# A graph network with experts on one core: edge stages in a fixed order, edge one-hots from ScalarE, and later work moved into them

## The chip, the cores and the metric

The kernel runs on one core of a Trainium2 chip. The metric is the device time of one execution in microseconds; the median of three runs stands for a kernel. A core has five engines with a queue of instructions each: PE (TensorE, matrix products into the accumulator memory PSUM; weight loads are its PEld row), DVE (VectorE), ACT (ScalarE), POOL (GpSimd, which also issues the indirect DMAs that gather rows by index) and SP (SyncE, which issues plain DMAs). [...]

## The reference

Nodes have 256 values each (3125 nodes); 53125 edges (`src`, `dst`) join them. Four layers follow each other, each added to its input, each on a layer norm:

```python
x = x + _L0_gnn_ref(_layernorm(x), edge_index, edge_weight, ...)
x = x + _L0_ffn_ref(_layernorm(x)[None], ...)[0]
x = x + _L1_gnn_ref(_layernorm(x), ..., src, dst, edge_type_200)
x = x + _L1_ffn_ref(_layernorm(x)[None], ...)[0]
```

Layer 0's graph part gives each edge four weights, `w = exp(-relu(score/20))`, where the score is a value of the edge's near node plus one of its far node plus a multiple of the edge's own value; a node receives the weighted mean of its neighbours' features (`pooled / row_sum`). Its experts part sends each node to the best two of 16 experts, each `silu(x w1) * (x w2)` times `w3`. Layer 1's graph part sums `(h[src] + rel_e) @ weight_neighbor * alpha` over the edges into a node, where `alpha = exp(leaky_relu(score))` divided by itself (so it is 1 up to rounding), takes a relu and adds one of two products of the node, by whether edges come in. Its last part gives every node a weight from a router vector, finds the 1561 nodes with the largest weights (`top_k` of half, less one), and for these adds a two-layer gelu network times the weight.

## The kernel before, in words

The kernel (a class, `_Kernel`, run by `run`, L1477) is written against a layer that adds the semaphores and, outside of fixed blocks, arranges the order of instructions on each engine by its own estimate of their times.

**Nodes** are 25 tiles of 128 (`NT`), `x` stays in SBUF. **Edges** are sorted by their near node into 25 buckets, one for each node tile, in 440 tiles of 128 edges (`sort_edges`, L310: `load_in`, `places`, `move`, `load`); 18 tiles make a bucket, handled in groups of `GRP` = 6 tiles, so there are 74 groups (`edge_groups`, L714). `load` (L578) keeps for each edge its far node's index, its row in the bucket and its value, and writes rows (and types, in layer 1) once more to DRAM as rows of bf16 (`wide`).

**An edge stage** is the same for both layers (`edge_stages`, L724, called through `pipelined`, L811). For each group:

- `gather` issues six indirect DMAs on POOL (L754) that fetch the far nodes' rows from a table in DRAM (`table0`, `table1`) into `rows` (3 buffers); at a bucket's head, `spread` has SP fetch the bucket's `wide` row to all partitions (L744); DVE makes `oh`, one-hots of edge by node, from `numbers` in PSUM and the edges' rows (L762); DVE makes the same turned over, `hot`, from `wide` (L771; in layer 1 two more, of relations).
- `message`: PE multiplies `hot` with near values (L780), DVE sums their three parts (L787), and the layer's `messages` makes weights and messages (L916 for layer 0; L1308 for layer 1, where it writes one-hots of the relation behind the gathered row, L1313, and ACT makes `ohw`, the one-hots times the weight, L1319).
- `add`: PE sums one-hots times messages into a bank of `ps_sums` (L798). After a bucket's last group, `acc` is that bank plus `more` (edges that overflowed, a DMA issued there, L804), and `finish` uses it (L933, L1324).

The stages stand one group apart: while group g is gathered, g-1 gets its messages and g-2 is summed. During layer 0's edges `pipelined` takes one piece of layer 1's sorting (`ranking`) per step, and `finish` calls `done` of `gate` (L966), which at the end of five buckets does their layer norm, writes them to `xtab`, and makes the experts' logits.

**After layer 0's edges**, `experts` (L989) routes the nodes, then runs 65 tiles of expert work with layer 1's `move` as filling, then combines: 50 gathers on POOL (L1170), each added to `x` by DVE (L1174). `relations_features` (L1181) then prepares layer 1's weights, norms all tiles and writes `table1` and `near1`; `load` fetches the sorted edges; `relations_edges` (L1272) is layer 1's edge stage. `depths` (L1367) then norms all tiles, makes the router's weights `wc`, turns them into a row, counts for each node how many weights are larger (49 comparisons over up to 3125 values, L1426), and runs the last network in blocks of four tiles (L1453, L1464).

PSUM is one pool for the whole kernel: tag A with 2 buffers of two banks, tag B with 4 of one.

## Time and profile before

| | us |
|---|---|
| median of 3 runs | 2635.79 (2631.52 to 2639.92) |
| the profiled execution's own time | 2845.15 |
| its span, first to last instruction | 2842.8 |
| mean granted PE clock | 0.822 of full speed |

| busy over the span | us | share | instructions |
|---|---|---|---|
| PE matmuls | 1878.6 | 66% | 7534 |
| PE weight loads | 1126.4 | 40% | 7534 |
| DVE | 1446.3 | 51% | 3397 |
| ACT | 390.7 | 14% | 1097 |
| POOL | 1167.4 | 41% | 1198 |

The profile is of one execution. A group's line names the line of the kernel, the engine, the operation, the tile written and those read, the count, then busy time and the mean of one in ns, and after a second bar the engine's idle time just before these instructions with what ended most of it. "issue" means that the profile shows nothing that was waited for, "remote" that what ended the wait isn't known to it. A line of the stretches gives length, busy time and count of PE, PEld, DVE, ACT and POOL, then PE's granted clock, the share of the DMA engines and GB/s. A line of waits gives the total, the number and the longest. The profiled execution took longer than the runs did; a sum of its durations is a sum in its own time.

### The profile page before, as it was taken

The page shows a single profiled execution, that of the slowest core. Times are in us where ns is not written, and L with a number is a line of the kernel's source. Part 1 is how long each engine was busy: PE and PEld are TensorE (multiplying, and loading weights), DVE is VectorE, ACT ScalarE, POOL GpSimd, SP SyncE. Part 2 cuts the span into 40 slices and gives each one's busy share as a digit, 9 for nine tenths or more (in the row PEclk, how much of TensorE's full clock was granted, in tenths as well). Part 3 has the DMA queues.
Part 4 walks back from the last instruction along what each step waited for, and adds up shares of the span by engine and source line. Part 5 has one row for each costly group of instructions (what it writes and reads, how often), then busy time and mean ns, then how long its engine had stood idle before and what let it go on. Part 6 is the DMA issues. An engine that isn't in the chain of part 4 may idle for free.

```text
span 2842.8 us, 24381 instructions
## 1 busy us (share of the span) xinstructions
PE 1878.6 (66%) x7534; PEld 1126.4 (40%) x7534; DVE 1446.3 (51%) x3397; ACT 390.7 (14%) x1097; POOL 1167.4 (41%) x1198
## 2 busy tenths in 40 slices
PE   3169554854544443399999991447878778785298
PEld 0024232543433332356666660323434334343166
DVE  4876225476665343644422224445655556549721
ACT  0000010010000000100112120112222222221012
POOL 4235306576654646034411115036666666650000
PEclk9999996676666667577799996768889888898599
DMA  2000325343444433144499982254545455431000
GB/s 83 0 3 5 104 89 137 93 130 112 115 100 114 116 100 101 49 150 130 131 316 318 317 291 84 87 156 131 148 129 148 130 142 149 128 85 34 8 21 18
DMA packets 258938, 334.04 MB, mean 118 GB/s; under 512 B 30861, under 2 KB 192407, under 8 KB 258807
## 3 DMA queue, kind: packets, MB, share of 16 engines
q1 hardware_dynamic: 197527, 191.26, 21.3%
q0 software_dynamic: 51920, 132.68, 17.6%
q10 hardware_dynamic: 9360, 8.52, 0.9%
q8 instruction: 61, 1.00, 0.1%
q14 instruction: 70, 0.57, 0.1%
HBM read 298.38 MB, written 33.98 MB: 117 GB/s over the span
## 4 chain that ended last, share of the span: by engine, by line
PE 39%; DVE 14%; issue 10%; POOL 9%; another core or an unknown queue 8%; DMA 4%; ACT 1%; SPq 0%; DVEq 0%; POOLq 0%; ACTq 0%
PE ps_sums L798 10%; PE ps_h L1130 9%; POOL rows L754 9%; PE ps_y L1147 4%; PE s_mv L560 3%; DVE cmp L1426 3%; PE ps_hid L1453 3%; PE ps_out L1464 3%; DMA rows<-table,s_idx 3%; DVE msg L926 2%; DVE hot L771 2%; PE ps_x_t L173 1%; PE ps_h_t L173 1%; PE ps_f L1264 1%
## 5 line engine op out<-in xcount | busy, mean ns | idle before, releaser
L754 POOL DMA_INDIRECT rows<-table,s_idx x880 | 848.6, 964 | 725.0 <-issue 240.4
L798 PE MATMUL ps_sums<-msg,oh 128*128 128x260 f32 x880 | 306.6, 519 | 261.8 <-DVE msg L926 143.1
L798 PE MATMUL ps_sums<-rows,ohw 128*128 128x457 f32 x880 | 414.0, 616 | 62.8 <-ACT ohw L1319 54.1
L798 PEld LDWEIGHTS ps_sums<-msg,oh 128*128 128x128 f32 x880 | 226.6, 265 | 325.1 <-issue 250.1
L560 PE MATMUL s_mv<-s_hv,s_hp 128*128 128x200 f16 (+1 forms) x832 | 246.8, 472 | 89.9 <-DVE s_hv L555 89.9
L798 PEld LDWEIGHTS ps_sums<-rows,ohw 128*128 128x128 f32 x880 | 179.0, 215 | 217.5 <-issue 149.6
L1130 PE MATMUL ps_h<-w,x_t 128*128 128x512 f32 x520 | 256.1, 638 | 0.0
L771 DVE TENSOR_SCALAR hot<-wide,pcols 128x768 bf16<-128x768 bf16 (+1 forms) x296 | 175.4, 597 | 73.9 <-PE ps_near L780 63.0
L560 PEld LDWEIGHTS <-s_hp 128*128 128x128 f16 x832 | 122.1, 147 | 208.7 <-issue 180.3
L762 DVE TENSOR_TENSOR oh<-ps_hold,s_row 128x768 f32<-128x768 f32 (+1 forms) x148 | 139.9, 946 | 125.7 <-remote 73.5
L1119 POOL DMA_INDIRECT xg<-xtab,who x65 | 61.9, 952 | 345.1 <-PE ps_x_t L173 302.6
L569 POOL DMA_INDIRECT s_tab<-s_rec,s_to x130 | 147.8, 1137 | 115.1 <-ACT s_rec L566 78.9
L780 PEld LDWEIGHTS <-hot 128*128 128x128 bf16 x1760 | 70.0, 98 | 212.3 <-issue 149.2
L1136 DVE TENSOR_TENSOR hid<-hid,ps_h 128x512 f32<-128x512 f32 x65 | 44.7, 688 | 210.3 <-ACT hid L1135 204.4
L1319 ACT ACTIVATE ohw<-oh,s 128x128 f32<-128x128 f32 x440 | 136.5, 388 | 106.6 <-DVE s L1282 75.2
L1130 PEld LDWEIGHTS ps_h<-w,x_t 128*128 128x128 f32 x520 | 102.8, 209 | 105.7 <-issue 105.5
L926 DVE TENSOR_TENSOR msg<-rows,ps_hold 128x1536 f32<-128x1536 f32 x74 | 128.1, 1731 | 2.0 <-ACT ps_hold L924 1.9
L787 DVE TENSOR_REDUCE near<-ps_near 128x24 f32<-128x72 f32 (+2 forms) x148 | 29.4, 198 | 190.3 <-remote 150.2
L1147 PE MATMUL ps_y<-w,h_t 128*128 128x256 f32 x520 | 122.9, 379 | 0.7 <-ACT h_t L175 0.7
L1147 PEld LDWEIGHTS ps_y<-w,h_t 128*128 128x128 f32 x520 | 98.7, 190 | 41.7 <-issue 30.6
L545 DVE TENSOR_TENSOR s_hp<-num_p,s_pp 128x1024 f16<-128x1024 f16 x104 | 71.8, 690 | 82.8 <-PE s_mv L560 81.4
L1313 DVE TENSOR_TENSOR rows<-ps_hold,s_val 128x1200 f32<-128x1200 f32 x74 | 101.1, 1367 | 6.1 <-PE ps_sums L798 6.1
(307 smaller groups left out, 2344.2 us busy)
## 6 DMA issues: line engine op xcount, KB each, us to landing
w<-in_L_ffn_w_dram SPq DMA_DIRECT2D x195, 512.0 KB
wide<-s_w SPq DMA_DIRECT2D x72, 576.0 KB
rows<-table,s_idx POOLq DMA_INDIRECT x880
ytab<-y ACTq DMA_DIRECT2D x65, 128.0 KB
sums<-sums_z SPq DMA_DIRECT2D x5, 1142.5 KB
more<-sums SPq DMA_DIRECT2D x25, 228.5 KB
sums<-sums_z SPq DMA_DIRECT2D x5, 650.0 KB
table<-f SPq DMA_DIRECT2D x5, 650.0 KB
```

Source lines behind the costliest of these rows:

```text
L560: nc.tensor.matmul(ps[:, : NK * V], hp[:, :, j], rec[:, :, :, j].rearrange("p k v -> p (k v)"), start=(j0 + j == 0), stop=(j0 + j == C - 1),)
L569: d = nc.gpsimd.indirect_dma_start(out=tab, out_offset=bass.IndirectOffsetOnAxis(ap=to[:, i : i + 1], axis=0), in_=out[:, k * CH * V : (k ...
L754: nc.gpsimd.indirect_dma_start(out=rows[:, j, :width], out_offset=None, in_=table, in_offset=bass.IndirectOffsetOnAxis(ap=st["idx"][:, k + ...
L762: nc.vector.tensor_tensor(oh[:, :n, :], numbers[:, None, :P].to_broadcast(sh), st["row"][:, k : k + n, None].to_broadcast(sh), op=OP.is_equal,
L771: nc.vector.tensor_scalar(t[:, : n // 2, :], w, at, None, op0=OP.is_equal)
L798: nc.tensor.matmul(ps[:, :W], oh[:, j, :], msg[:, j, :], start=(head and j == 0), stop=(last and j == n - 1),)
L926: nc.vector.tensor_tensor(msg[:, :n, :HO].rearrange("p j (h o) -> p j h o", o=O), rows[:, :n, :HO].rearrange("p j (h o) -> p j h o", o=O), ...
L1130: nc.tensor.matmul(ph[:, i * HID : (i + 1) * HID], xt[:, c, :], w12[:, i, c, :], start=(c == 0), stop=(c == C - 1),)
L1147: nc.tensor.matmul(py[:, :D], ht[:, c, :], w3[:, c, :], start=(c == 0), stop=(c == HC - 1))
L1313: nc.vector.tensor_tensor(rows[:, :n, R0:], self.numbers[:, None, :R].to_broadcast(sh), st["val"][:, k : k + n, None].to_broadcast(sh), op ...
L1319: nc.scalar.activation(ow[:, j, :], oh[:, j, :], AF.Copy, scale=s[:, 1, j : j + 1])
L1426: nc.vector.tensor_scalar(cmp[:, s:e], wrow[:, s:e], w, None, op0=op, op1=OP.add, accum_out=rank[:, t, i : i + 1],)
```

## The change: what it does

1. **Edge stages.** `edges` takes the place of `edge_stages` and `pipelined`, and inside `tc.manual_schedule()` every engine keeps the order in which the code issues its instructions. A step g issues: the spread of group g+2 (now for each group, two rows of 128 with 8 of padding side by side, so that a group is one run of 1584 bytes), the gathers of g, the closing of a bucket whose last group was g-3, the one-hots and near products of g, the message and the sums of g-1, and a piece of other work, up to 2.2 us by the numbers that the pieces yield. A bucket's `more` is loaded with its first spread. `finish` is a generator and goes on in half steps.
2. **One-hots.** DVE's `oh` comparison goes. ACT makes |row - node| for each tile (`Abs`); in layer 0 a Relu of 1 minus that is the one-hot; in layer 1 the Relu has scale -alpha and bias alpha, and so carries the weight.
3. **Layer 1's relation one-hots** (`prepare`) are written right after the group's gather is issued. `rows` has 4 buffers in layer 1, `oh` 3 in layer 0.
4. **Filling.** The sort's pieces yield 2.6; `gate`'s work is cut into pieces that are queued behind it. The last layer's norm, router weights and counts (`router`, `route`) leave `depths` and become pieces of layer 1's edge stage; a count over all nodes is split by when the nodes are finished. Its weights are loaded ahead of that stage.
5. **Layer 1's features.** Weights are prepared ahead of `experts`; norm and `table1` of four tiles follow as soon as these are combined.
6. **PSUM** is opened anew for each part; in the edge stages it holds two near banks, two separate banks of sums, one held bank and three others.

```diff
     def load():
...
+            wide = [
+                self.dram.tile([MT // 2, 2 * P + 8], BF16, name=f"{name}_w{i}")
+                for i in range(1 + (not bits))
+            ]
...
+        def spread(g):
+            b, k, n, head = groups[g][:4]
+            wide[g] = []
+            for i, w in enumerate(st["wide"]):
+
+                t = pool.tile([P, G // 2, 2 * P + 8], BF16, name=f"wide{i}", bufs=3)
+                src = w[k // 2 : (k + n) // 2, :].rearrange("(o k) r -> o (k r)", o=1)
+                nc.sync.dma_start(
+                    t[:, : n // 2, :].rearrange("p k r -> p (k r)"),
+                    src.to_broadcast([P, n // 2 * (2 * P + 8)]),
+                )
+                wide[g].append(t[:, : n // 2, : 2 * P])
             if head:
-                now[b] = [spread(i, b) for i in range(len(st["wide"]))]
-            rows = pool.tile([P, G, into], F32, name="rows", bufs=3)
+                more[b] = pool.tile([P, W], F32, name="more")
+                nc.sync.dma_start(more[b], sums[b])
+
+        def gather(g):
+            k, n = groups[g][1:3]
+            rows = pool.tile([P, G, into], F32, name="rows", bufs=self.rows_bufs)
...
-            oh = pool.tile([P, G, P], F32, name="oh", bufs=3)
-            nc.vector.tensor_tensor(
-                oh[:, :n, :], numbers[:, None, :P].to_broadcast(sh),
-                st["row"][:, k : k + n, None].to_broadcast(sh), op=OP.is_equal,
-            )
...
+            far = pool.tile([P, G, P], F32, name="off", bufs=2)
+            for j in range(n):
+                nc.scalar.activation(
+                    far[:, j, :], self.iota[:, :P], AF.Abs, scale=-1.0,
+                    bias=st["row"][:, k + j : k + j + 1],
+                )
+            pe = self.ps("near", "ps_near")
...
+        def close(b):
+            acc = pool.tile([P, W], F32, name="acc")
+            nc.vector.tensor_add(acc, bank.pop(b)[:, :W], more.pop(b))
+            yield from finish(b, acc)
...
+        with tc.manual_schedule():
+            spread(0)
+            spread(1)
+            for g in range(len(groups) + 3):
+                if g + 2 < len(groups):
+                    spread(g + 2)
+                if g < len(groups):
+                    rows = gather(g)
+                if g >= 3 and groups[g - 3][4]:
+                    closers.append(close(groups[g - 3][0]))
+                go_on()
+                if g < len(groups):
+                    live[g] = rows, *hots(g)
+                    if prepare:
+                        prepare(*groups[g][1:3], rows)
+                if 0 <= g - 1 < len(groups):
+                    message(g - 1)
+                go_on()
+                piece(2.2)
+            while closers:
+                go_on()
+            piece(1e9)
...
-            def messages(k, n, rows, near, oh):
+            def messages(k, n, rows, near, off):
+                oh = pool.tile([P, G, P], F32, name="oh", bufs=self.oh_bufs)
+                nc.scalar.activation(oh[:, :n, :], off[:, :n, :], AF.Relu, bias=1.0, scale=-1.0)
...
-                done(b)
...
+                self.queue.append(done(b))
+                yield
...
-    def experts(self, fill):
+    def experts(self, fill, done):
...
+                done(t)
...
+            ends = list(range(4, NT - 4, 4)) + [NT - 3, NT]
+
+            def done(b):
+                if b + 1 not in ends:
+                    return
+                i = ends.index(b + 1)
+                t0, t1 = ends[i - 1] if i else 0, b + 1
+                self.norm_tiles(self.h1, t0, t1)
...
+                nc.vector.tensor_scalar(s[:, 2, :n], s[:, 1, :n], -1.0, None, op0=OP.mult)
                 ow = pool.tile([P, G, P], F32, name="ohw", bufs=3)
                 for j in range(n):
                     nc.scalar.activation(
-                        ow[:, j, :], oh[:, j, :], AF.Copy, scale=s[:, 1, j : j + 1]
+                        ow[:, j, :], oh[:, j, :], AF.Relu,
+                        bias=s[:, 1, j : j + 1], scale=s[:, 2, j : j + 1],
                     )
...
+        def route(b):
+            if b + 1 not in ends:
+                return
+            i = ends.index(b + 1)
+            t0, t1 = ends[i - 1] if i else 0, b + 1
+            for _ in self.norm_pieces(z, t0, t1):
+                yield 1.2
...
+            end = min(N, t1 * P)
+            for t in range(t0):
+                count(t, t0 * P, end, OP.is_gt, 3 + i)
+                if t % 3 == 2:
+                    yield 2.2
+            for t in range(t0, t1):
+                lo, hi = t * P, min(N, (t + 1) * P)
+                count(t, 0, lo, OP.is_ge, 0)
+                count(t, lo, end, OP.is_gt, 1)
...
+                yield 2.2
...
+        general = dict(A=2, B=4)
+        at_edges = dict(near=2, sums=2, hold=1, B=3)
...
+                    self.rows_bufs, self.oh_bufs = 3, 3
                     self.heads_edges(st, ranking, self.gate(pool))
-                with tc.tile_pool(name="move1", bufs=1) as moves:
-                    self.experts([lambda f=f: f(moves) for f in steps])
-        self.relations_features()
-        self.relations_edges(load())
-        self.depths()
+                with self.banks(**general):
+                    features = self.relations_features()
+                    with tc.tile_pool(name="move1", bufs=1) as moves:
+                        self.experts([lambda f=f: f(moves) for f in steps], next(features))
+                        next(features, None)
+                    st = load()
+        with tc.tile_pool(name="route", bufs=1) as pool:
+            with self.banks(**at_edges):
+                self.router(pool)
+                self.rows_bufs, self.oh_bufs = 4, 2
+                self.relations_edges(st)
+            with self.banks(**general):
+                self.depths()
```

## The prediction

> **What bounds the kernel now.** I read the page's busy shares first, then the mean of each stage, then what the gathers cost and wait for, then who waits longest in the two edge stages. No engine is full over the span:
>
> ```profile
> PE 1878.6 (66%) x7534; PEld 1126.4 (40%) x7534; DVE 1446.3 (51%) x3397; ACT 390.7 (14%) x1097; POOL 1167.4 (41%) x1198
> ```
>
> So each stage has its own limit. Stages, from the busy times by stretch: layer 0's edges, the experts alone, combining plus layer 1's tables, layer 1's edges, and the last layer.
>
> ```profile
> 429.00:1169.00 740.00, 384.03 (x1586) 282.81 (x1586) 410.72 (x967) 51.54 (x190) 432.66 (x440) 0.68 0.40 109
> ...
> 1420.00:1718.00 298.00, 295.38 (x1120) 185.53 (x1118) 78.33 (x153) 61.33 (x103) 42.54 (x45) 1.00 0.90 299
> 1718.00:1871.00 153.00, 41.37 (x186) 29.46 (x186) 67.89 (x200) 9.86 (x27) 47.65 (x51) 0.68 0.29 90
> 1871.00:2557.00 686.00, 525.91 (x2486) 266.08 (x2487) 379.81 (x959) 171.97 (x587) 415.89 (x440) 0.86 0.50 137
> 2557.00:2843.00 286.00, 192.64 (x716) 129.52 (x714) 148.32 (x313) 50.12 (x83) 0.29 (x1) 0.85 0.06 20
> ```
>
> Columns: length, then busy time of PE, weight loads, DVE, ACT, POOL, then granted clock, DMA share, GB/s. The experts alone are PE at full clock; the change leaves them. In the edge stages nothing is full, yet POOL's floor is high. Back to back its gathers start 1.25 us apart (0.95 and an idle 0.30 that waits for nothing):
>
> ```profile
> 2107.24 0.94 POOL L754 DMA_INDIRECT rows<-table,s_idx  x1 [0.30 <-issue]
> 2108.49 0.95 POOL L754 DMA_INDIRECT rows<-table,s_idx  x1 [0.30 <-issue]
> ```
>
> 440 gathers make 550 us per layer, 7.5 us for a group of six. Layer 0 takes 740, layer 1 686. What lies above the floor is in the groups of each edge stage (first layer 0's, then layer 1's):
>
> ```profile
> L754 POOL DMA_INDIRECT rows<-table,s_idx x440 | 432.7, 983 | 381.5 <-DVE msg L926 161.5 <-issue 123.1 <-DVE near0p L651 85.7
> ```
> ```profile
> L754 POOL DMA_INDIRECT rows<-table,s_idx x429 | 405.6, 945 | 255.1 <-issue 114.3 <-PE ps_sums L798 73.8 <-PE ps_near L780 61.5
> ```
>
> POOL waits because its three row buffers come free late: after DVE's messages in layer 0 (161.5 us), after PE's sums and near values in layer 1 (135.3). Behind that stand DVE waits with no releaser that the profile shows:
>
> ```profile
> DVE oh L762 <- remote: 73.5, 9, 14.0
> DVE acc L806 <- remote: 70.8, 6, 18.4
> ...
> DVE near L787 <- remote: 38.7, 6, 12.3
> ```
> ```profile
> DVE near L787 <- remote: 111.6, 24, 7.4
> ```
>
> 183 us in layer 0, 112 in layer 1. In each case PE's result is late, though its instructions look done or crawl: in layer 1 the tiny near matmuls, 25 ns apart at first, suddenly come 0.70 us apart:
>
> ```profile
> 2120.87 0.16 PE L780 MATMUL ps_near<-near1p,hot 128*128 128x3 bf16 x1 [0.48 <-issue]
> ...
> 2121.57 0.16 PE L780 MATMUL ps_near<-rel_p,hot 128*128 128x3 bf16 x1 [0.54 <-issue]
> ```
>
> The profiled execution took 2845.15 us (span 2842.8); the runs have a median of 2635.79, 209 less. I take these stray PE waits for most of that difference: they are of its size, sit on the engine with 15068 of 24381 instructions, and do not appear where PE is full (experts). That choice decides the forecast.
>
> [...] beside scans (L437) gathers take up to 1.54 us instead of 0.95; layer 0's mean is 983 ns against 945. [...] Here the waits for a single gather landing are 2.5 to 2.9 us. [...]
>
> **The change part by part.** *One-hots on ScalarE.* DVE loses 148 comparisons of 945 ns (140 us). ACT gains 880 sizes of 128x128 and 74 Relus of 128x768; in layer 1 the weighted copy becomes a Relu. [...] The weighted copy is 388 ns in the trace[...]. [...] The nearest row (388 ns for 128x128) as the high end makes it 2.3 a group more, 5.2, still covered. The gain side, DVE's 140 us, stands in DVE's sums below.
>
> *Layer 0 in fixed order.* Per group DVE: hot 0.60, near 0.23, three small ops with their latencies and Exp 1.2, messages 1.73, a third of a closing (0.43+0.17+0.41+0.42) 0.5, so 4.3; a ranking piece (0.38+0.20+1.02+0.59+0.59) 2.8: 7.1, just below POOL's 7.5. Sums on PE 2.9 to 5.2 by clock. So POOL paces: 550, + 17 for gathers slowed by scans (432.7 - 440x0.945), + 3 until the first lands, + 10 from the last gather to the last sum, + 10 for the two lumps of ranking that exceed a step (some 16 and 25 small ops in one piece; the slack of a third row buffer swallows about 10 us of each). 590 against 740: **-150**. What becomes late next is POOL itself.
>
> *Layer 1 in fixed order, router brought in, fourth row buffer.* DVE: three hots 1.79, the relation one-hots 1.37 (both moved ahead of the message), near/score/weight chain 1.9 with Exp in it, closing (0.64+0.41+0.42+0.30+0.96)/3 = 0.9: less about 0.3 of overlap 5.7. A router piece adds 2.2: 7.9, just above POOL. The yields name 156 us of pieces; the first come at step 18, so some 57 steps have one and about 30 us remain after the loop. 16x7.5 + 58x7.9 = 578, + 8 start, + 10 flush = 596 against 686: **-90**. PE has 0.5 near + 4.7 sums + 1.4 closing = 6.6, below both. The neg added before each Relu (0.15) is in the chain.
>
> *Router's place.* After the edges DVE spent 133 us (120.3 busy) on norms, 88.9 us of counts and the rest, with PE doing two blocks of hidden values. Then PE ran 153 us. PE's own work there is 89.8 + 87.5 + 7.5 = 185. After: that 185, + 10 until the banks are free, + 4 for the last store; the 30 us of router hide under the first hidden blocks. 199 against 286: **-87**.
>
> *Layer 1's table made while experts are combined.* Combining is 50 gathers x 1.25 = 63 us plus landing; DVE per tile 2x0.48+0.60+0.41+0.43 = 2.4 against POOL's 2.5, so 72 with square-root waits. The last three tiles: norm 3, transposes and products 5.6, copy and store 4.5: 13; landing of the table and near parts 5. 90 against 153: -63. Preparation moves ahead of the routing (w3a work 5.4 us and small ops): +8 if not hidden. The last layer's 2 MB of weights now stand on SP's queue ahead of the first spreads: +5. Net **-50**. SP's spreads per group (222 issues of 0.36 us in place of 75, up to 3 a step with `more`) have 7.5 us each step, POOL gets one mask ahead of layer 1's gathers, and `more` is now queued early instead of behind its own accumulator; 1584-byte runs replace 512-byte ones, which I count as nothing.
>
> Sum: 150+90+87+50 = 377; 2845 - 377 = 2468 in profiled time. For the runs: if the 209 us are stray waits of the edge stages, these stages take 740+686-209 = 1217 there now and 590+596 = 1186 after, -31; with 87 and 50 that is 168: 2636 - 168 = **2468**. Both ways meet because the new floor has no stray waits in it.
>
> **Rivals.** (1) The stray waits are real in runs too. The profile's quiet experts speak for my reading, the waits' length (18 us, ending after the gathers drain) against it. Half of the 209 outside the edges: 2636 - (31+105+137) = 2363; all spread evenly: 377x0.927 = 349, 2287. (2) A fixed order cannot step around a late result: DVE stands behind Exp and PE each step, with the router piece and the next hots queued behind it and PE's near values and then POOL's buffers waiting for those. At +0.9 us a step in layer 1 and +0.4 in layer 0 (67+30): 2565. The small chain of 1.9 us per step, with ACT's sizes ahead of Exp, speaks for it. (3) Slower: the relation one-hots are written into the row tile right after its gather is issued; if that waits for the gather to land and buffers don't decouple, a layer-1 step is 7.5+2.5+2 = 12: 74x4.1 = 303 more, 2771. It decides from 2.3 us a step upward (168/74). Against it: four buffers give 30 us, and the use from gather to last sum is some 26. (4) The compiler's order was as good and only moves count: 2636-137 = 2499, inside my own range.
>
> **How the numbers follow.** My forecast and (4) 0.53, from 2430 to 2510; (1) 0.28; (2) 0.12; (3) 0.05; no change 0.02. Leaving out the full form of (1) and the worst of (2) and (3) gives 2340 to 2580. Faster by over 0.3% (about what runs can tell) 0.93, within 0.02, slower 0.05.
>
> **What would show it.** Right: gathers 1.25 us apart with few waits, edge stages near 590 each in the profile, under 40 us from the last sums to DVE's last count, table gathers starting about 90 us after combining begins, the profiled time closer to the runs' than now. Wrong: gathers waiting for messages or sums again, DVE idle on Exp or DMA, or profiled gains of 370 that the runs show too.

## The result, and the profile after

The changed kernel takes 2776.9 us (2775.1 to 2783.7, four runs) where the kernel before takes 2635.8 (2631.5 to 2639.9): a ratio of 1.054, 95% interval 1.0516 to 1.0565. It is slower by 141 us; 2468 was forecast.

The runs fell on several chips, and a time can only be read beside that of the kernel before on the same chip. That time is of two kinds: 2636 to 2643 us (the comparison above, the second and the fourth group of experiments), called the first kind of chip below, and 2844 to 2905 (the other three groups), called the second. Every ratio is against the kernel before on the same chip, and stage times are compared within a kind only. Each group ran on one chip and no two groups on the same, so it is not shown that the chip itself makes the kind, and not something else that lasted as long as a group. The profiled execution of the kernel before (2845.15 us) has the time of the second kind, that of the changed kernel (2776.95) the time of its own runs on the first.

Engine totals of the changed kernel, and its stages: layer 0's edges, experts with combining and tables, layer 1's edges, the last layer (columns as before: length, busy time of PE, weight loads, DVE, ACT and POOL, granted clock, DMA share, GB/s).

```profile
PE 1951.5 (70%) x7534; PEld 1172.1 (42%) x7534; DVE 1423.3 (51%) x3509; ACT 754.0 (27%) x2073; POOL 1163.7 (42%) x1198
```
```profile
431.00:1053.00 622.00, 391.33 (x1586) 289.88 (x1586) 393.37 (x909) 231.79 (x704) 425.14 (x440) 0.73 0.48 131
1053.00:1721.00 668.00, 571.61 (x2100) 363.29 (x2099) 268.66 (x661) 100.75 (x199) 180.11 (x183) 0.82 0.63 204
1721.00:2535.00 814.00, 572.88 (x2500) 295.56 (x2500) 431.19 (x1174) 353.71 (x1044) 419.07 (x440) 0.81 0.42 116
2535.00:2775.00 240.00, 191.05 (x702) 127.39 (x700) 95.49 (x253) 48.28 (x82) 0.00 (x0) 0.90 0.04 14
```

Layer 1's edges take 814 us though no engine is busy for more than 573 of them. The groups of gathers, layer 0's and then layer 1's:

```profile
L816 POOL DMA_INDIRECT rows<-table,s_idx x440 | 425.4, 967 | 264.3 <-issue 120.6 <-DVE near0p L690 86.0 <-DVE msg L1006 44.2
```
```profile
L816 POOL DMA_INDIRECT rows<-table,s_idx x440 | 419.1, 952 | 377.3 <-PE ps_sums L866 196.4 <-issue 114.2 <-DVE ln_st L185 22.7
```

In layer 0 POOL sets the pace for the most part, as forecast: only 44 us of waits for messages are left (86 lie ahead of its first gather). In layer 1 it waits 196 us for PE's sums to give a row buffer back. Who is late there is told by the waits of that stage:

```profile
ACT s L1375 <- DVE s L1374: 280.2, 42, 11.1
PEld ps_sums L866 <- ACT ohw L1418: 196.7, 174, 5.3
POOL rows L816 <- PE ps_sums L866: 196.4, 39, 9.0
...
DVE agg L1454 <- PE ps_rel L1441: 160.9, 23, 9.2
DVE s L1376 <- ACT s L1375: 139.7, 74, 6.9
...
ACT ct L1435 <- PE ps_cnt L1431: 104.3, 23, 6.3
...
PE ps_near L846 <- DVE hot L830: 76.4, 83, 4.9
```

They form a ring: POOL waits for PE, PE for ACT, ACT for DVE, DVE for PE. Two members belong to the closing of a bucket and come 23 times each: DVE's addition (`agg`) that needs PE's product of the counts (`ps_rel`), and ACT's copies of the counts (`ct`) that PE turns over for it (`ps_cnt`). One bucket shows how they fit; first DVE, then ACT, in order of time (start, length, instruction, idle time before it):

```profile
2002.11 0.17 DVE L1374 SCALAR_TENSOR_TENSOR s<-s 128x6 f32<-128x6 f32 x1
2006.40 0.19 DVE L1376 RECIPROCAL s<-s 128x6 f32<-128x6 f32 x1 [4.13 <-ACT s L1375]
...
2008.23 0.08 DVE L1554 DVE_READ_ACCUMULATOR eq<-wrow,wc,after 128x1 f32 x1
2015.27 0.42 DVE L1454 TENSOR_TENSOR agg<-acc,ps_rel 128x256 f32<-128x256 f32 x1 [6.96 <-PE ps_rel L1441]
...
2017.91 1.64 DVE L830 TENSOR_SCALAR hot<-wide,pcols 128x768 bf16<-128x768 bf16 x3
```
```profile
2003.82 0.42 ACT L1435 COPY ct<-ps_cnt 128x128 f32<-128x128 f32 x2 [3.78 <-PE ps_cnt L1431]
2004.14 0.38 ACT L207 COPY x_t<-ps_x_t 128x256 f32<-128x256 f32 x1
2004.40 1.87 ACT L838 ACTIVATE off<-iota,s_row 128x128 f32<-128x128 f32 x6
2006.17 0.20 ACT L1375 ACTIVATE s<-s 128x6 f32<-128x6 f32 x1
2007.25 2.42 ACT L1418 ACTIVATE ohw<-off,s 128x128 f32<-128x128 f32 x6 [0.88 <-DVE s L1415]
```

At 2002.3 DVE has the scores ready, but Exp is late: ACT's copies of the counts stand ahead of it, with the next six sizes between, and wait for PE, whose turning of them stands behind six tiles of sums. Exp runs at 2006.2, the weighted one-hots until 2009.7, and only with them the next sums. Behind these PE makes the bucket's last products, and DVE, from 2008.3 on, stands at the addition that needs them until 2015.3. The next group's one-hots are queued behind that addition and start at 2017.9, so PE has no near products meanwhile, and the ring goes round once more. From 2008.3 to 2015.3 the trace has no other instruction of DVE: one-hots that need nothing from PE's last products lie still behind the addition for 7 us. The first gathers of four groups in a row show what it costs:

```profile
1998.69 1.02 POOL L816 DMA_INDIRECT rows<-table,s_idx  x1 [7.53 <-PE ps_sums L866]
...
2006.27 0.95 POOL L816 DMA_INDIRECT rows<-table,s_idx  x1 [0.30 <-issue]
...
2014.63 0.94 POOL L816 DMA_INDIRECT rows<-table,s_idx  x1 [1.17 <-PE ps_sums L866]
...
2029.45 0.94 POOL L816 DMA_INDIRECT rows<-table,s_idx  x1 [7.49 <-PE ps_sums L866]
```

From one group to the next it is 7.6, 8.4 and 14.8 us, so this bucket takes 30.8 us where six gathers a group would need 22.5. Twelve of the 24 buckets with three groups are like it (30 to 33 us). The first three take 22.5, one takes 27.8, and eight, two after every fifth node tile, take about 37.5: there the router's pieces add waits of the same sort, DVE's for ACT's square root (L190, 30.0 us in four waits) and ACT's for PE's turned weights (L1538, 20.1 in four). All 24 lie 228 us above 22.5 each, and 196 us of this stage POOL waits for PE's sums.

### The profile page after: what moved, and what is told of

The parts are those of the page before. It is cut to its first block, busy times and chain, and to the rows that moved or that the text cites. A ratio compares the mean times of both kernels' runs of the same rounds, so it can differ in the third digit from the quotient of the medians.

```text
span 2775.2 us, 25627 instructions
## 1 busy us (share of the span) xinstructions
PE 1951.5 (70%) x7534; PEld 1172.1 (42%) x7534; DVE 1423.3 (51%) x3509; ACT 754.0 (27%) x2073; POOL 1163.7 (42%) x1198
## 3 DMA queue, kind: packets, MB, share of 16 engines
q1 hardware_dynamic: 143880, 192.63, 22.5%
## 5 line engine op out<-in xcount | busy, mean ns | idle before, releaser
L866 PE MATMUL ps_sums<-rows,ohw 128*128 128x457 f32 x880 | 456.0, 678 | 156.9 <-ACT ohw L1418 124.4
L866 PE MATMUL ps_sums<-msg,oh 128*128 128x260 f32 x880 | 325.7, 544 | 182.5 <-ACT off L838 109.4
L866 PEld LDWEIGHTS ps_sums<-rows,ohw 128*128 128x128 f32 x880 | 201.2, 237 | 363.6 <-ACT ohw L1418 196.7
L866 PEld LDWEIGHTS ps_sums<-msg,oh 128*128 128x128 f32 x880 | 237.3, 278 | 239.9 <-ACT off L838 112.2
L838 ACT ACTIVATE off<-iota,s_row 128x128 f32<-128x128 f32 x880 | 272.0, 389 | 1.5
L1418 ACT ACTIVATE ohw<-off,s 128x128 f32<-128x128 f32 x440 | 177.3, 481 | 51.4 <-DVE s L1415 51.4
L830 DVE TENSOR_SCALAR hot<-wide,pcols 128x768 bf16<-128x768 bf16 (+1 forms) x296 | 165.1, 598 | 7.0 <-DMA wide<-s_w 7.0
L1514 DVE TENSOR_SCALAR_CACHE_REDUCE cmp<-wrow,wc 128x640 bf16<-128x640 f32 (+16 forms) x122 | 107.1, 878 | 6.0 <-ACT wrow L1542 2.8
```

What stands on the lines that cost most here:

```text
L830: nc.vector.tensor_scalar(t[:, : n // 2, :], wide[g][min(i, 1)], at, None, op0=OP.is_equal)
L838: nc.scalar.activation(far[:, j, :], self.iota[:, :P], AF.Abs, scale=-1.0, bias=st["row"][:, k + j : k + j + 1],)
L866: nc.tensor.matmul(bank[b][:, :W], oh[:, j, :], msg[:, j, :], start=(head and j == 0), stop=(last and j == n - 1),)
L1418: nc.scalar.activation(ow[:, j, :], oh[:, j, :], AF.Relu, bias=s[:, 1, j : j + 1], scale=s[:, 2, j : j + 1],)
L1514: nc.vector.tensor_scalar(cmp[:, s:e], wrow[:, s:e], wc[:, t : t + 1], None, op0=op, op1=OP.add, accum_out=rank[:, t, i : i + 1],)
```

## The experiments

There are five groups of experiments, and the time of the kernel before on the same chip stands with each. The expectations weigh explanations under short names. Theory Closing: the place of a bucket's closing in the fixed order makes the loss. Theory Exp: each step's Exp stands behind ACT's six sizes. Theory ScalarE: its one-hots are too slow for the sums. Theory Order, from the third group on: any fixed order loses, wherever the closing stands. A step has two places at which closings go on, one ahead of the group's one-hots and one behind the message; each `yield` moves what follows it on to the next of these places, by a half step.

**First group (before at 2905 us): where does layer 1's time go?** Three edits, and the changed kernel with its order set free. The closing moved, in two steps; the second includes the first:

```diff
+                yield
                 yield
                 xt = self.x[:, t, :]
                 v = pool.tile([P, D], F32, name="agg")
```
```diff
-                for i, (r0, n) in enumerate(rc):
-                    nc.scalar.copy(ct[:n, i, :], pt[:n, i * P : (i + 1) * P])
-                ht = self.transposed(self.h1[:, t, :], D, "x_t")
+                px = self.ps_b("ps_x_t")
+                for i in range(C):
+                    nc.tensor.transpose(
+                        px[:, i * P : (i + 1) * P], self.h1[:, t, i * P : (i + 1) * P], self.ident
+                    )
                 yield
                 yield
+                for i, (r0, n) in enumerate(rc):
+                    nc.scalar.copy(ct[:n, i, :], pt[:n, i * P : (i + 1) * P])
+                ht = pool.tile([P, C, P], F32, name="x_t")
+                nc.scalar.copy(ht.rearrange("p c q -> p (c q)"), px[:, :D])
                 pr = self.ps_b("ps_rel")
```

> The changed kernel with one more half step between PE's last products of a bucket in layer 1 (relations, loop) and DVE's use of them; DVE's addition (agg) then stands behind the next group's one-hots and message instead of ahead of them. Theory Closing (DVE waits 7.2 us for PE at each of 25 buckets, with the next one-hots queued behind, so a bucket takes 30.7 us where POOL needs 22.5): layer 1's edges fall from 814 to about 640 us, total 2777 to about 2605 (2570 to 2650). Theory Exp (each step's Exp stands behind ACT's six sizes) and theory ScalarE (its one-hots are too slow for the sums): under 30 us less, about 2750 or more.

> As the one before, and ACT's copies of the counts and of the turned node values in layer 1 also moved, from ahead of the next group's sizes and Exp to behind its weighted one-hots. Theory Closing: ACT's idle 3.8 us per bucket ahead of Exp goes too; the gathers of layer 1 come 7.5 us a step apart in nearly every step, layer 1's edges about 590 us, total about 2560 (2530 to 2600). Theory Exp: as the changed kernel, within 40 us. Theory ScalarE: same.

The other two issue the six sizes behind the message of the group before, and take the block away that fixes the order (which the kernel before does not have):

```diff
...
                 if 0 <= g - 1 < len(groups):
                     message(g - 1)
+                if g < len(groups):
+                    sizes(g)
                 go_on()
```

> The changed kernel with ACT's six sizes of a group issued after the message of the group before, so that Exp no longer stands behind them. Theory Exp: DVE's 124 us of waiting for Exp in layer 1 (63 waits) shrink to some 20 and the total falls by about 100, to 2680. Theory Closing: the waits at a bucket's closing remain (7.5 and 14.8 of a bucket's 7.5, 8.4, 14.8), only the 0.9 in the middle step can go: 25 x 0.9 = 22 less, 2755 (2730 to 2775). Theory ScalarE: no change.

```diff
-        with tc.manual_schedule():
+        if True:
```

> The changed kernel without the block that fixes the order of the edge stages; ScalarE's one-hots, buffers and moved work stay as they are, and the order is again arranged by estimated times. Theory Closing (the fixed order is at fault): 2636 or less, about 2560. Theory ScalarE (sums wait for the one-hots whatever the order): stays above 2700.

Measured: 2862.3 for the addition alone (0.987, 0.980 to 0.995), 2822.5 with the copies (0.973, 0.966 to 0.981), 2942.6 for the sizes (1.017, 1.008 to 1.025), 2807.0 for the free order (0.968, 0.960 to 0.975). The totals that I had expected assumed the other kind of chip and can't be set beside these, but the stages can be set beside each other. Layer 1's edges took 740 us with the addition moved, 708 with both, 823 with the sizes moved, 748 in the free order. With the sizes moved DVE still waits 88.6 us for Exp and longest at the closing, and the stage stays by far the longest of the four. The changed kernel itself has 836 on another chip of this kind (third group), so theory Exp, which foresaw about 100 us less, falls. In the free order layer 1's edges take 40 us longer here than in the fixed one with both parts of the closing moved.

**Second group (before at 2641): layer 0 alone, and the one-hots alone.** Two kernels end after layer 0's edges; one puts ScalarE's one-hots into the kernel before, in layer 1 only; one takes them out of the changed kernel.

```diff
                     self.heads_edges(st, ranking, self.gate(pool))
+                    for t in range(self.NT):
+                        n = min(P, self.N - t * P)
+                        nc.sync.dma_start(self.out[t * P : t * P + n, :], self.x[:n, t, :])
+                    return
```

> The kernel before, ended when layer 0's edges are done (everything after is left out; x as it then is goes to the output). Its time shows where the 209 us lie by which the profiled execution of the kernel before exceeds its runs. If they are stray waits of PE in layer 0's edges: the profiled execution at about 1185, the runs at about 1065 (120 us less; more if layer 0 holds all of them). If they lie in layer 1 or in the experts: runs and profile agree within 20 us.

> The changed kernel, ended at the same point (everything after layer 0's edges is left out). In its profile layer 0's edges took 622 us against 740 before. Theory Stray waits: its runs and its profile agree, near 1065, and stand within 30 us of the other's runs, so that layer 0 has gained little or nothing and layer 1 has lost what the total shows. If the 118 us of the profiles are real: it runs 100 us or more ahead of the other.

```diff
+            if others:
+                for j in range(n):
+                    nc.scalar.activation(
+                        oh[:, j, :], self.iota[:, :P], AF.Abs, scale=-1.0,
+                        bias=st["row"][:, k + j : k + j + 1],
+                    )
+            else:
+                nc.vector.tensor_tensor(
...
+                nc.vector.tensor_scalar(s[:, 2, :n], s[:, 1, :n], -1.0, None, op0=OP.mult)
...
-                        ow[:, j, :], oh[:, j, :], AF.Copy, scale=s[:, 1, j : j + 1]
+                        ow[:, j, :], oh[:, j, :], AF.Relu,
+                        bias=s[:, 1, j : j + 1], scale=s[:, 2, j : j + 1],
```

> The kernel before with one part of the change alone, in layer 1: the one-hots of edges by nodes come from ScalarE (sizes, then a Relu with the weight), no fixed order, DVE's comparison of 945 ns a group left out there. Theory Closing: the one-hots by themselves cost nothing, the total stays within 1% of 2636 or falls up to 50. Theory ScalarE: it becomes slower by 50 us or more, as the sums wait for them.

> The changed kernel with the one-hots back on VectorE in both layers (comparison of 945 ns a group, the weighted copy in layer 1 on ScalarE), the fixed order and the moves kept. Theory Closing: the waits at a bucket's closing stay; DVE has 0.95 more in each step and ACT 1.75 less ahead of Exp: about as the changed kernel, 2750 to 2830. Theory ScalarE: the loss goes, 2640 or less.

Measured: the kernel before needs 1034.3 us to the end of layer 0's edges, in its profiled execution (1034.4) as in its runs; the changed one 1054.7. The stage of the kernel before, cut there:

```profile
431.00:1025.00 594.00, 371.38 (x1586) 276.29 (x1586) 406.80 (x955) 52.08 (x190) 433.86 (x440) 0.73 0.51 141
```

Its layer 0 takes 594 us where the profile shown with the prediction had 740: being profiled does not make the stage long, and that profile has the times of the other kind of chip. Layer 0 was near POOL's pace already (440 gathers 1.25 us apart are 550 us), and the changed kernel is 20 us later at its end. I had expected about 1065 for both; the first was 31 less.

ScalarE's one-hots alone in layer 1 give 2630.6 against 2641.1 (0.9955, 0.994 to 0.997): in the order arranged by estimates they cost nothing and bring some 10 us; as the cause of the whole loss theory ScalarE falls. Apart from layer 1's edges, that kernel's stages are those of the kernel before on this kind of chip:

```profile
429.00:1029.00 600.00, 374.95 (x1586) 278.26 (x1586) 410.75 (x966) 52.04 (x190) 435.45 (x440) 0.72 0.49 134
1029.00:1725.00 696.00, 552.40 (x2098) 353.69 (x2098) 272.64 (x648) 99.08 (x193) 179.15 (x182) 0.83 0.60 193
1725.00:2340.00 615.00, 510.07 (x2488) 262.61 (x2488) 331.87 (x960) 337.91 (x1027) 416.61 (x440) 0.89 0.56 152
2340.00:2624.00 284.00, 191.36 (x714) 129.68 (x712) 148.41 (x313) 50.26 (x83) 0.29 (x1) 0.85 0.06 20
```

With 2636 in all, layer 1's edges of the kernel before are left with about 628 (2634 of span less 429, 597, 696 and 284). So the 141 us are: layer 0 +25, experts and tables -28, layer 1 +186, last layer -44, by subtraction within 5 us. The changed kernel with DVE's one-hots took 2754.5 (1.041, 1.038 to 1.044): 646 in layer 0, 760 in layer 1, its DVE still idle 125 us at that same addition:

```profile
1754.00:2514.00 760.00, 541.17 (x2499) 282.94 (x2500) 479.80 (x1175) 182.06 (x604) 416.92 (x440) 0.84 0.47 124
```
```profile
DVE agg L1449 <- PE ps_rel L1436: 124.6, 23, 6.3
```

Most of the loss survives without ScalarE's one-hots: layer 1 stays about 132 us above the 628 of the kernel before. But not all of it: as long as the closing stands where it is, layer 1's edges are 54 us longer with ScalarE's one-hots than with DVE's (814 against 760), while layer 0's are 24 us shorter (622 against 646). So the one-hots, which cost nothing in the arranged order, add to the ring in the fixed one; with the closing moved (fourth group) they stay and the loss is gone.

**Third group (before at 2844): the changed kernel beside its variants.**

> The changed kernel itself, so that the others of this group stand beside it on one chip. If the difference between the two profiled executions (2845 us for the kernel before against 2636 in its runs) was one of chips and not of profiling: on a chip where the kernel before takes 2630 to 2650, this takes 2770 to 2785; on one where that takes 2880 to 2920, this takes 2900 to 2950 and its edge stages are longer by over 100 us.

> The changed kernel with layer 1's closing issued later (DVE's addition behind the next group's one-hots and message, ACT's copies behind the next weighted one-hots). Theory Closing: 190 to 220 us less than the changed kernel on the same chip where PE's results come on time (layer 1's edges at about 600), 2560 to 2590. Theory Order (any fixed order loses, wherever the closing stands): less than 100 us gained.

> The changed kernel without the block that fixes the order. Theory Closing: layer 1's edges within 40 us of the variant with the closing moved, total 2560 to 2620. Theory Order: clearly faster than that variant, by 50 us or more.

```diff
-        with tc.manual_schedule():
+        with tc.manual_schedule() if others else ExitStack():
```

> The variant with the closing moved, and layer 0's edges in the order arranged by estimated times, layer 1's in the fixed one. If each is the better order for its layer: layer 0's edges at 600 or less in place of 622, the total 20 to 40 us below the variant with the closing moved, about 2540, and below the kernel before. If the fixed order was no loss in layer 0: same as that variant.

In the last of these edits `others` is empty in layer 0, so that only layer 1 keeps the fixed order.

Measured: 2944.9 for the changed kernel (1.034, 1.031 to 1.038), 2819.5 with the closing moved (0.991, 0.987 to 0.995), 2780.7 in the free order (0.976, 0.972 to 0.980) and 2768.9 with layer 0 alone set free (0.971, 0.967 to 0.976). The changed kernel is that of the first comparison, the chip is not. Its edge stages here (layer 0, then layer 1), and a wait in layer 0's stage that has no releaser known to the profile:

```profile
430.00:1185.00 755.00, 386.58 (x1586) 287.53 (x1586) 393.21 (x911) 232.46 (x704) 420.88 (x440) 0.69 0.40 108
...
1865.00:2701.00 836.00, 578.88 (x2500) 298.56 (x2500) 431.29 (x1176) 354.14 (x1045) 418.58 (x440) 0.80 0.41 113
```
```profile
DVE near L858 <- remote: 173.5, 18, 16.0
```

Layer 0 is 133 us longer than on the other kind; such waits are what the prediction called stray. Moving the closing takes layer 1's edges from 836 to 711, and the total by 125 us where 190 to 220 were expected: on this kind of chip other waits remain, and the kernel before has 686 too. In the free order layer 1's edges take 734 here, 23 more than in the fixed order with the closing moved, and the kernel that fixes layer 1 alone is slightly ahead of the free one (intervals of 0.967 to 0.976 and 0.972 to 0.980). Theory Order falls for layer 1; for layer 0 the free order is better (708 against 755).

**Fourth group (before at 2643): the same on the first kind of chip.**

> The changed kernel with layer 1's closing issued later. If the chip is like that of the first comparison (kernel before at 2630 to 2650): theory Closing: layer 1's edges at 600 to 630, total 2570 to 2600, 0.98 of the kernel before; theory Order: 2680 or more. If it is like the other two (2840 to 2910): 0.97 to 0.99 as there.

> The changed kernel without the block that fixes the order. Theory Closing: within 1% of the variant with the closing moved in layer 1's edges; layer 0's edges at about 597 in place of 622 as in the kernel before; total 2530 to 2590 on a chip with the kernel before at 2636, 0.97 on the others.

> Layer 0's edges in the arranged order, layer 1's in the fixed one with the closing moved. On either kind of chip the best of the variants so far: 0.96 to 0.975 of the kernel before, 20 to 40 us under the variant with both layers fixed.

```diff
             while closers:
                 go_on()
+            if prepare:
+                while next(self.queue[-1]) != 2.25:
+                    pass
             piece(1e9)
...
-            yield 2.2
+            yield 2.25
```

> As the one before, and after the last step of layer 1 the last two node tiles' norm, weights and PE's turning of them are issued ahead of the counts that are left over. If PE's late start in the last layer (its first product came 41 us after the closing's last, behind that turning) sets the end: 20 to 35 us less. If the counts set it, since no output can be formed before the last count: less than 15 us.

Measured, with the stages of the profiled executions:

| kernel | median | ratio (95%) | layer 0 | experts, tables | layer 1 | last |
|---|---|---|---|---|---|---|
| changed (first comparison) | 2776.9 | 1.054 (1.052 to 1.057) | 622 | 668 | 814 | 240 |
| closing moved | 2559.1 | 0.968 (0.966 to 0.970) | 623 | 678 | 588 | 240 |
| and layer 0 free | 2522.6 | 0.955 (0.953 to 0.956) | 581 | 673 | 586 | 240 |
| and the last turning early | 2507.0 | 0.949 (0.947 to 0.951) | 583 | 673 | 588 | 228 |
| no fixed order at all | 2475.6 | 0.935 (0.933 to 0.938) | 583 | 677 | 572 | 214 |

Two edits in the place of a few instructions, none removed, take 226 us off one stage (the changed kernel itself was not run on this chip; ratios are compared, 0.968 and 1.054). The stage with the closing moved, and its gathers:

```profile
1732.00:2320.00 588.00, 497.57 (x2499) 267.14 (x2500) 428.74 (x1176) 352.76 (x1044) 419.12 (x440) 0.91 0.57 161
```
```profile
L816 POOL DMA_INDIRECT rows<-table,s_idx x440 | 419.1, 953 | 155.1 <-issue 115.5 <-DVE near1t L691 11.3 <-PE ps_cnt L1431 11.1
```

Of the 196 us behind PE's sums 6 are left, and the gathers run at their floor: 7.5 us a group nearly everywhere, 22.5 to 25.9 us a bucket. DVE's wait at the addition is 23.7 us in 18 times and for Exp 43.0:

```profile
DVE s L1376 <- ACT s L1375: 43.0, 74, 3.3
...
DVE agg L1461 <- PE ps_rel L1447: 23.7, 18, 3.1
```

PE's busy time falls too, without an instruction less: 498 us against 573, at a granted clock of 0.91 against 0.81. Why the clock differs no run here tests.

On this kind of chip the free order beats all. Against the kernel with the closing moved, layer 1 is 16 us shorter, layer 0 is 40 and the last layer 26. In layer 0 the same pattern shows. The waits of DVE for the gate's logits in that stage, in the changed kernel and then in its free order:

```profile
DVE logits L1066 <- PE ps_logit L1063: 71.0, 23, 6.8
```
```profile
DVE logits L1066 <- PE ps_logit L1063: 3.8, 5, 1.1
```

The last turning moved early brought 16 us (2522.6 to 2507.0; 12 in the last layer's stage), which lies between the two expectations, nearer to that of the counts.

**Fifth group (before at 2891): the addition alone, and the gate.** The first kernel has the same edit as the first of the first group; it was to show on the first kind of chip what the addition is worth by itself. The second moves layer 1's closing and cuts the gate's work in layer 0 so that PE's turning of a tile, its copy and logits, and DVE's addition are one step apart.

> The changed kernel with only DVE's addition of layer 1's closing issued later; ACT's copies stay ahead of the next sizes and Exp. By the waits of the changed kernel (DVE 7.2 us and ACT 4 us a bucket, of 8.2 us that a bucket is too long): if they overlap, most of the 218 us go with the addition alone and layer 1's edges take 610 to 640; if each counts by itself, about 690. On the chips with the kernel before at 2840 or more, about 740 as in the first group.

```diff
-                    turned[t] = self.transposed(xn[:, t, :], D, "x_t")
-                if t > t0:
-                    xt = turned.pop(t - 1)
...
+                if t - 2 in summed:
+                    pl = summed.pop(t - 2)
+                    nc.vector.tensor_add(self.logits[:, t - 2, :], pl[:, :NE], self.gate_b)
+                if t - 1 in turned:
+                    px = turned.pop(t - 1)
...
-                    yield 1.0
+                    yield 2.2
```

> The changed kernel with layer 1's closing moved, and in layer 0 the gate's work cut so that a tile's turning on PE, its copy on ACT with the logits on PE, and DVE's addition of the logits lie one step apart each. Both layers stay in the fixed order. If layer 0's loss has the same cause as layer 1's: layer 0's edges fall from 623 to 585 to 600, total about 2530 (0.957) on a chip with the kernel before at 2640. If it comes from the lumps of ranking or from ScalarE: 615 or more, total as the variant with the closing moved, 2559 (0.968).

Measured: 2860.7 (0.997, 0.995 to 1.000) and 2799.0 (0.971, 0.965 to 0.978); layer 1's edges 740 with the addition alone, as in the first group, 704 with both; layer 0's 764 and 743. The chip was of the second kind. There the addition is worth about 96 us of layer 1's 836 and the copies 32 to 36 more; on the first kind the two were never taken apart. Cutting the gate differently won 21 us (764 to 743, one profile each) of the 47 that the free order wins in layer 0 on such chips (755 to 708 in the third group), while seven of DVE's waits at the logits, 101.5 us, are now of the kind without a known releaser. The medians agree: with layer 1's closing moved alone the other two chips of this kind gave 2819.5 and 2822.5, against 2799.0. So the gate's place is, as it seems, part of layer 0's loss. That it is all of it is not shown, and the forecast of 585 to 600 was for the first kind of chip, on which this kernel did not run.

## Why the prediction was wrong, point by point

**The forecast.** It was 2468 us, from 2340 to 2580, and gave a slower kernel a chance of 0.05; 2776.9 was measured.

**The choice on the 209 us.** Half right. The number was: the edges of the kernel before take about 597 + 628 = 1225 in its runs, and the prediction worked with 1217. The cause was wrong: profiling does not make the waits, since on the second kind of chip the runs have them too (2844 and more). Rival (1), that they are in the runs of the first comparison, falls. That the prediction's two ways both lead to 2468 supports nothing: 2845 - 377 and 2636 - (377 - 209) are one sum, with the 209 taken off at the start or at the end.

**One-hots on ScalarE.** Right in the price. From the 388 ns of the weighted copy the prediction put ACT at 5.2 us at most for a group of layer 1. In the group shown above, six sizes (389 ns each on average) take 1.87 us, Exp 0.20 and six weighted Relus (481 ns each) 2.42: 4.5 together; ACT's 353.7 us of busy time in the stage are 4.8 a group. That POOL covers them holds in the arranged order, where they cost nothing alone (2630.6 us against 2641.1), and not in the fixed order, where layer 1 took 54 us less without them.

**Layer 0 in fixed order, 590.** Off by 32 us: 622. Without the fixed order the same code takes 583, so the sum of the work was about right. What it put at nothing are waits between engines: DVE waits 71.0 us at PE's logits, 3.8 in the free order. How much of the 32 these are is open.

**Layer 1 in fixed order, 596.** This is the step that failed: 814. The prediction added up what each engine has to do in a step (7.9 for DVE, 6.6 for PE, at most 5.2 for ACT) and took the longest. It entered the closing as 0.9 us of DVE's work a step, but not the place where it stands: behind PE's last products, ahead of the next one-hots. There DVE waits 160.9 us for PE at the addition, and ACT 104.3 us at the copies, which stand ahead of the next Exp; both waits were put at nothing. With the closing moved the stage takes 588, in the free order 572, so the sum of 596 was about right for an order without them.

**Rival (2)** named this mechanism, a fixed order that cannot step around a late result, with DVE behind PE and ACT. It sized it at 0.9 us a step from Exp and the sizes; the stage lost (814 - 596)/74 = 2.9, and most of it through the closing, which the rival did not look at. Exp's wait is real (139.7 us), and ACT's sizes have a share in the loss (814 against 760 without them, in the second group), but moving the sizes alone left the stage at 823 on the second kind of chip, where the changed kernel has 836. **Rival (3)** came nearest in time (2771) for the wrong reason: `prepare` never waits (its 74 one-hots have 0.0 us of idle time before them), but its deciding point, 2.3 us a step, was passed by the other one; that the total fits is luck. **Rival (4)** was right that the arranged order is as good as the fixed one: the kernel before is near the floor with it (594 and about 628), and the changed kernel takes 2475.6 us in it, where the rival said 2499. It did not foresee that the fixed order would be worse, and the moves brought 72 us in the changed kernel (28 and 44), not 137.

**The last layer, 199.** It took 240. PE's own work was right (183 us from its first product to its last, for 185); the 51 us between the last sums and that product were sized 10. PE turns the last nodes' weights only when DVE has made them (28.5 us for one of two waits), and DVE makes them behind the leftover counts of the group before, so that product waits until 2585.6. Of the 41 us, 12 came back with that turning ahead of the counts, 26 in the free order.

**Combining and tables, -50.** Measured -28 against the kernel before on this kind of chip (696), -34 against the profile that the prediction started from (702).

**Together.** The four misses, 32 + 218 + 41 + 16 = 307, lead from 2468 to 2775. Without the one block that fixes the order the change takes 2475.6. That this is so near 2468 is in part luck: against the forecast its stages are 7 and 24 us shorter in the two edge stages, 25 and 15 longer in the other two.

## What to carry to other kernels

When an order is fixed by hand, busy time per step is not enough: for each instruction that reads another engine's result, ask what is queued ahead of the producer on that engine and what is queued behind the reader on its own. Here ACT's copies were issued in the half step of their producer and DVE's addition in the next one, and both made two queues wait for each other; one or two half steps later the addition waited 23.7 us in place of 160.9, and these few lines were worth 226 us of a stage. A fixed order is not bad in itself: with the closing moved, layer 1's edges took 588 us against 572 in the order arranged by estimates on the first kind of chip, and 708 and 711 against 748 and 734 on the second. Compare a profile's own time with the runs before reading its waits: where they differ by 8%, find out whether the two ran on different chips before explaining the waits.

## What was not expected of the hardware

The kernel before takes 2636 to 2643 us on some chips and 2844 to 2905 on others, the changed one 2777 and 2945. Nearly all of the difference lies in the edge stages (changed kernel: 622 and 814 against 755 and 836; its other stages 668 and 240 against 680 and 240). There DVE waits for near values with no releaser known to the profile: 173.5 us in 18 waits in layer 0 of the changed kernel. In the variant with the closing moved, on that chip, neither PE nor DVE has a record from 616.0 to 621.3 us. What holds them up was not found. It changes what an edit is worth: the change is 1.054 on one kind and 1.034 on the other, and the variant with the closing moved 0.968 and 0.973 to 0.991. On the first kind the free order is the best of the variants (0.935); on one chip of the second, layer 1 fixed with the closing moved and layer 0 free is as good or slightly better (0.971 against 0.976).
